# Row statistics dealt out piece by piece, token loads moved to the head of each product, weighting one step later, and output splits placed behind P1's copies

## The chip, the core and the metric

The kernel runs on one core of a Trainium2 chip. The metric is the device time of one execution in microseconds (us). Before the change three runs took 2683.50, 2684.97 and 2689.05 us, with a median of 2684.97.

## The reference

Input x has 2 sequences of 2048 tokens with 2048 features, all in fp32. The output is the residual of x with an attention layer and a routed feed-forward layer on the normalised tokens:

```python
xn = _layernorm(x, axis=-1)
# attention, one head of width 512
qkv = jnp.einsum('bsc,cf->bsf', xn, Wqkv) + bqkv          # 2048 -> 3 x 512
attn = softmax(jnp.einsum('bqd,bkd->bqk', q, k) * scale)
att = jnp.einsum('bqd,dc->bqc', jnp.einsum('bqk,bkd->bqd', attn, v), Wo) + bo
# feed-forward, 64 experts of rank 8
scores = (xn @ Wq_w.T) @ keys.T                           # 2048 -> 16 -> 64
top_vals, top_idx = jax.lax.top_k(scores, 16)             # softmax over the 16, scattered to a gate of 64
z = (xn @ A_w.T) * gate                                   # 2048 -> 512, 8 features to an expert
ffn = z @ B_w.T * SCALING                                 # 512 -> 2048
return x + att + ffn
```

## The kernel before, in words

**Tiling.** Tokens are taken in 8 blocks of 512 (four blocks to a sequence), each block as four tiles of 128 rows. Each fp32 product is made from three passes: an operand is cast to fp32r (`hi`, `split_hi`, L122, on ScalarE, ACT), what the cast dropped is kept as a second operand (`lo`, `split_lo`, L125, on VectorE, DVE), and three of the four combinations are accumulated in PSUM (`product`, L130). So each weight piece and each activation goes through a DMA, a cast on ACT and a subtraction on DVE before TensorE (PE) can use it. Seven PSUM banks serve the products (`acc`), one the small transposes (`misc`).

**Stages.** (1) `first_block` and the features of block 0: 12 feature tiles of 48 matmuls, 128x512 each (to 204 us). (2) Block 1: `values(1)` (L285) makes the values and the router's input in two halves h, each over eight weight pieces c2 with 24 matmuls of 128x264, in four banks; then 12 feature tiles (to 399 us). (3) Blocks 2 to 7 in pairs, `PAIRS` j = 1 to 3, by a seven-product scheme over the pair: phases P1, P2, P6, P5, P3, P7, P4 in this order (`phase`, L740). A phase has seven items: six feature tiles of 24 matmuls (5.44 us at the steady pitch of 227 ns) and one item "V" for the values. (4) Attention in 128 steps of 12 + 12 matmuls: `score(s)`, and after a lag `soft` (exponential and split) and `weigh`. (5) The output projection, 8 groups q of seven `STEPS`, again P1 to P4 by name, in `multiply` and `combine`, with `moving` bringing the output weights.

**Normalising.** Layernorm needs each row's mean and reciprocal deviation. `stats_steps` (L201) makes the steps for one block: for each of four row tiles it loads the rows (`xs`, L214) and takes `bn_stats` (L195) and an aggregate (L198) on DVE; then `finish_` copies the means into `mr` (L220), prepares the variance (L188) on DVE, raises it to -0.5 on GpSimd (POOL, L189), transposes `mr` on PE (L223), copies it out of PSUM on ACT (L225), writes it to DRAM (L227) and reads it back spread over all partitions (`mb`, L229). `norm` (L243 on, blocks 0 and 1) and `x_steps` (L608 loads of `xq`, L615 and L616 the arithmetic, later blocks) apply it to the transposed tokens.

**What sets the order of work.** Each engine works through its instructions in the order in which the scheduler puts them. `last` holds the latest instruction recorded on a queue under a key, and `behind(...)` issues what is in its body after that one. SyncE (SP) issues all the DMAs, so its queue is the one DMA queue. Weights of the phases are fetched two pieces ahead (`fetch`, L579; its DMA is L592), and a `fetch` sets `last["sp"]` and `last["dve"]`. The side work of a phase is a list of steps that `beside` (L647) returns; `phase` deals it out evenly over the seven items, each step behind SP, PE and DVE. There the token loads of the next product are steps like the others. In P2 and P3 item V comes first; its results feed `router` and `choose` (top 16 of 64 by repeated maxima on DVE, L447) behind items 0 and 1. In `values(1)` a statistics step comes with every third piece; `values_out` copies a half's banks out on DVE (`vs`, L125). Feature tiles of blocks 0 and 1 take side steps from the table `todo`. Steps are merged evenly by `mixed`.

**Attention's lag.** `LAG` = 20: step s scores tile s, softens tile s-18 and weighs tile s-20. A block is 16 steps. `maxes(blk)` takes a block's row maxima on DVE (to `mq`, L947), `spread` transports them with one matmul (L957). `combos` (L1076 on DVE, inputs `xz`) makes sums for the output stage in the same loop.

**Output stage.** P1's result `ps` is copied to `u` by ACT (L1139), and P2 then accumulates onto the same bank. In the last group of the first column half (q = NG-1), `moving(1, ...)` loads the second half's output weights, and the list `more` holds their splits (`wb`, from `wo<-tw_d`, L122 and L125), made a step after their loads.

Of the kernel before, what the change touches and what calls it, by code (L numbers as in the profile page):

```python
# [8 lines left out]
F32 = mybir.dt.float32  # L9
# [7 lines left out]
P = 128  # L17
C = 2048
# [13 lines left out]
LAG = 20  # L32
# [31 lines left out]
def attn_ffn_kernel(ctx: ExitStack, tc, x, xT, wq, wv, wob, bqk, bv, bo, keysT, out):  # L64
# [136 lines left out]
    def stats_steps(i, r, cols, out):  # L201

        part = {}

        def rows(t):
            if t == 0:
                part["mv"] = const.tile([P, NT, 2], F32, name="mv", bufs=2)
            mv = part["mv"]
            st = const.tile([P, 4, 6], F32, name="st6", bufs=2)
            parts = 0  # L210
            for c in range(C // cols):
                xs = r([P, cols], F32, "xs")
                r0 = i * T + t * P
                nc.sync.dma_start(xs, x[r0 : r0 + P, c * cols : (c + 1) * cols])  # L214
                parts = row_stats(mv[:, t, :], [xs], parts, st)

        def finish_():
            mv = part["mv"]
            mr = const.tile([P, 2, NT], F32, name="mr", bufs=2)
            nc.vector.tensor_copy(mr[:, 0, :], mv[:, :, 0])  # L220
            rstd(mr[:, 1, :], mv[:, :, 1], NT)
            pt = misc([2 * NT, P])
            nc.tensor.transpose(pt, mr.rearrange("p a t -> p (a t)"), ident)  # L223
            ts = const.tile([2 * NT, P], F32, name="ts", bufs=1)
            nc.scalar.copy(ts, pt)  # L225
            sd = dram.tile([2 * NT, P], F32, name=f"sd{i}")
            nc.sync.dma_start(sd, ts)  # L227
            mb = r_mb([P, 2, T], F32, "mb")
            nc.sync.dma_start(  # L229
                mb.rearrange("p a t -> p (a t)"),  # L230
                sd.rearrange("a b -> (a b)").unsqueeze(0).to_broadcast([P, 2 * T]),
            )
            out[i] = mb

        return [lambda t=t: rows(t) for t in range(NT)] + [finish_]
# [49 lines left out]
    def values(i, xn, steps):  # L285
        qr = router_in()
        for h in range(2):
            ps = [acc() for t in range(NT)]
            for c2 in range(NCH // 2):
                wh = wv_piece(h, c2)  # L290
                for cc in range(2):
                    c = 2 * c2 + cc
                    for t in range(NT):
                        sl = slice(t * P, (t + 1) * P)
                        product(
                            ps[t][:, :VH], lambda a: xn[c][:, a, sl], lambda b: wh[:, b, cc, :],
                            c == 0, c == NCH - 1,
                        )
                if steps and c2 % 3 == 1:
                    with behind("sp", "pe"):  # L300
                        steps.pop(0)()
            flush()
            for t in range(NT):
                values_out(i, t, h, r_ev, qr, ps[t])
        return qr
# [341 lines left out]
    def beside(j, ph):  # L647
# [4 lines left out]
        if ph == "P1":  # L652
            t3 = sum_steps(j, nc.vector, b01, b11, b01, ALU.subtract)
            if j > PAIRS[0]:
                return mixed(
                    split_steps(j, "P2", *b10), x_steps(j, *b01)[1], x_steps(j, *b11)[1], t3
                )
            q = [x_steps(j, *b) for b in (b10, b01, b11)]
            loads = [st for k in range(3) for st in q[k][0]]
            return loads + mixed(q[0][1], split_steps(j, "P2", *b10)) + mixed(q[1][1], q[2][1])  # L660
        if ph == "P2":
            t3 = sum_steps(j, nc.vector, b01, b11, b01, ALU.subtract) if j == PAIRS[0] else []
            return mixed(
                t3, sum_steps(j, nc.vector, b00, b01, b00, ALU.add), split_steps(j, "P6", *b00)
            )
        if ph == "P6":
            return mixed(
                sum_steps(j, nc.vector, b10, b10, b00, ALU.subtract),
                sum_steps(j, nc.vector, b00, b11, b00, ALU.subtract), split_steps(j, "P5", *b00),
                s0[:NT] if more else [],  # L670
            )
        if ph == "P5":
            steps = mixed(split_steps(j, "P3", *b11), s1[:NT] if more else [])
            return steps[:2] + s0[NT:] + steps[2:] if more else steps
        if ph == "P3":
            n = x_steps(j + 1, *b00) if more else ([], [])
            steps = mixed(split_steps(j, "P7", *b01), n[1][:2])
            return n[0] + (s1[NT:] if more else []) + steps
        if ph == "P7":
            n = x_steps(j + 1, *b10) if more else ([], [])  # L680
            return n[0] + mixed(split_steps(j, "P4", *b10), n[1][:2])
        if more:
            return (
                x_steps(j + 1, *b01)[0] + x_steps(j + 1, *b11)[0] + x_steps(j + 1, *b00)[1][2:]
                + mixed(split_steps(j + 1, "P1", *b00), x_steps(j + 1, *b10)[1][2:])
            )
        return []
# [52 lines left out]
    def phase(j, ph, n):  # L740

        steps = beside(j, ph)
# [64 lines left out]
    for i in range(2):  # L807
        if i:
            s2 = stats_steps(2, r_xs, 1024, mbs)
            qr = values(i, xn, s2[:NT])  # L810
# [6 lines left out]
        if i == 0:  # L817
            s1 = stats_steps(1, r_xs, 1024, mbs)
            todo = {3: s1[:2], 4: s1[2:4], 7: s1[4:]}
        else:  # L820
            s3, q = stats_steps(3, r_xs, 1024, mbs), x_steps(1, 0, 0)
            todo = {1: s3[:2] + s2[4:], 2: s3[2:4], 4: q[0], 5: s3[4:], 6: q[1][:2], 7: q[1][2:]}
# [311 lines left out]
    def combine(q, step, t, ps):  # L1134
        if step == "P1":
# [3 lines left out]
            nc.scalar.copy(u, ps)  # L1139
# [39 lines left out]
    for s in range(NSTEP + LAG):  # L1179
# [10 lines left out]
        if LAG <= s < LAG + 8 * 2 * ND and s % 8 == 4:  # L1190
            n = (s - LAG) // 8
# [8 lines left out]
        if 0 <= s - LAG + 2 < NSTEP:  # L1200
            soft(s - LAG + 2)
# [32 lines left out]
    for q in range(2 * NG):  # L1234
# [4 lines left out]
        for n, step in enumerate(STEPS):  # L1239
# [16 lines left out]
            m = n + 7 * q - 7 * (NG - 1)  # L1256
            if 0 <= m <= 7:
                for _, split in more:
                    split()
# [45 lines left out]
```

## Time and profile before

| | us |
|---|---|
| runs, median of three | 2684.97 |
| the profiled execution | 2687.31 |
| its span | 2685.5 |
| PE busy | 2637.3 |
| DVE busy | 1804.4 |
| ACT busy | 859.8 |
| POOL busy | 571.7 |

The mean granted TensorE clock was 0.992 of full speed. The chain of work that ended last was 75% PE by its own instructions, 1% DVE, 1% issue. Of PE's instructions the three-pass products at L130 hold 52% of that chain, the output products at L1127 22%. DMA moved 530 MB, 198 GB/s on the mean; a 512-KB load of tokens (`xq`) landed 6.2 us after its issue by the median, and a 512-KB weight piece of the phases after 3.6 to 3.9 us.

How to read it: a row of the waits says which PE instruction waited for whose result, for how long in total, how often, and the longest. In a timeline a row is a run of like instructions on one engine, with its start, its length, and in brackets how long the engine was idle before it and what ended the idling. A row can hold several instructions (x3), and its times then include the gaps between them.

### The profile page before, as it was taken

What the parts mean: (1) busy time and instruction counts of PE and PEld (TensorE: products, weight loads), DVE (VectorE), ACT (ScalarE), POOL (GpSimd) and SP (SyncE); (2) the same over time, 40 slices, a digit from 0 to 9 for tenths busy, and PEclk for the clock granted to TensorE, in tenths of its full rate; (3) what the DMA queues carried; (4) which work ended last, traced back from release to release, by engine and by line L of the source; (5) the groups of instructions that cost most, each with busy time, mean ns of one, the idle gap of its engine ahead of it and who ended that gap; (6) DMA issues with size and microseconds to landing.
All of it is one profiled execution on the core that took longest, in us unless ns stands there. A gap on an engine that the chain in (4) does not pass through costs nothing.

```text
span 2685.5 us, 33806 instructions
## 1 busy us (share of the span) xinstructions
PE 2637.3 (98%) x12875; PEld 2230.5 (83%) x12875; DVE 1804.4 (67%) x2481; ACT 859.8 (32%) x1271; POOL 571.7 (21%) x355
## 2 busy tenths in 40 slices
PE   8997999999999999999999999999999999989999
PEld 8887888888888888888888888888878888878887
DVE  7567647967878678756544775456657776786675
ACT  4332323323333333323233433334434222232221
POOL 2321420001000000000100101000000655565554
PEclk9998999999999999999999999999999999999999
DMA  7676874667646684536835476534457544664543
GB/s 261 233 271 229 280 261 168 228 211 266 216 143 211 220 291 158 167 118 212 289 114 179 156 259 243 197 116 142 145 180 247 163 163 160 200 202 163 181 155 105
DMA packets 243363, 530.42 MB, mean 198 GB/s; under 512 B 21576, under 2 KB 87168, under 8 KB 243200
## 3 DMA queue, kind: packets, MB, share of 16 engines
q1 hardware_dynamic: 243200, 528.26, 58.5%
q8 instruction: 101, 1.65, 0.2%
q14 instruction: 62, 0.51, 0.1%
HBM read 393.80 MB, written 134.38 MB: 197 GB/s over the span
## 4 chain that ended last, share of the span: by engine, by line
PE 75%; DVE 1%; issue 1%; DMA 0%; POOL 0%; ACT 0%; SPq 0%; DVEq 0%; POOLq 0%; ACTq 0%
PE acc L130 52%; PE acc L1127 22%; DVE wb L125 0%; DMA xz<-oz_d 0%; DMA wo<-tw_d 0%; DVE s L125 0%; PE misc L957 0%; DVE xz L1078 0%; DVE xo L1116 0%; POOL mr L189 0%; PE misc L997 0%; PE misc L998 0%; PE misc L435 0%; DVE xz L1076 0%; DVE xz L1079 0%
## 5 line engine op out<-in xcount | busy, mean ns | idle before, releaser
L130 PE MATMUL acc<-t,pw 128*128 128x512 f32 x3024 | 697.0, 391 | 1.1 <-DVE pw L125 1.1
L130 PEld LDWEIGHTS acc<-t,pw 128*128 128x128 f32 x3024 | 567.6, 188 | 119.4 <-DVE pw L125 1.3
L1127 PE MATMUL acc<-wb,s 128*128 128x512 f32 x2688 | 612.3, 390 | 8.6 <-ACT u L1139 8.6
L1127 PEld LDWEIGHTS acc<-wb,s 128*128 128x128 f32 x2688 | 506.0, 188 | 114.3 <-ACT u L1139 9.0
L130 PE MATMUL acc<-ph,vt 128*128 128x512 f32 x1536 | 369.9, 391 | 0.6 <-DVE ph L125 0.6
L130 PE MATMUL acc<-qt,kt 128*128 128x512 f32 x1536 | 366.1, 389 | 0.0
L130 PEld LDWEIGHTS acc<-ph,vt 128*128 128x128 f32 x1536 | 289.2, 189 | 63.2 <-DVE ph L125 1.4
L130 PEld LDWEIGHTS acc<-qt,kt 128*128 128x128 f32 x1536 | 288.1, 188 | 60.2 <-issue 0.2
L1111 POOL TENSOR_TENSOR xo<-xo,bo_bc 128x512 f32<-128x512 f32 x128 | 205.9, 1615 | 590.5 <-DMA xo<-in_x 555.0
L122 ACT CAST pw<-pw 128x1024 fp32r<-128x1024 f32 (+1 forms) x168 | 177.8, 1058 | 414.5 <-PE acc L130 295.3
L125 DVE TENSOR_TENSOR pw<-pw 128x1024 fp32r<-128x1024 f32 (+1 forms) x168 | 210.8, 1255 | 84.9 <-ACT pw L122 79.7
L130 PE MATMUL acc<-xh,wh 128*128 128x512 f32 x1152 | 263.7, 390 | 0.0
L130 PEld LDWEIGHTS acc<-xh,wh 128*128 128x128 f32 x1152 | 215.6, 188 | 45.0
L130 PEld LDWEIGHTS acc<-pw,t 128*128 128x128 f32 x2016 | 245.7, 188 | 4.4 <-DVE pw L125 3.2
L130 PE MATMUL acc<-pw,t 128*128 128x264 f32 x2016 | 246.4, 283 | 3.0 <-DVE pw L125 3.0
L122 ACT CAST s<-xz 128x1024 fp32r<-128x1024 f32 x112 | 118.0, 1054 | 378.2 <-PE acc L1127 311.6
L125 DVE TENSOR_TENSOR s<-xz,s 128x1024 fp32r<-128x1024 f32 x112 | 165.7, 1479 | 49.2 <-ACT s L122 49.1
L125 DVE TENSOR_TENSOR ph<-sp,ph 128x512 fp32r<-128x512 f32 x128 | 94.2, 745 | 102.4 <-ACT ph L122 101.9
L929 DVE TENSOR_TENSOR M<-M,sp 128x512 f32<-128x512 f32 x112 | 80.1, 715 | 121.3 <-ACT sp L923 121.2
L505 POOL TENSOR_TENSOR zt<-zt,g 128x512 f32<-128x512 f32 x24 | 38.1, 1595 | 477.1 <-DMA g<-gd 242.7
L923 ACT COPY sp<-acc 128x512 f32<-128x512 f32 x128 | 74.7, 585 | 201.1 <-PE acc L130 201.0
L125 DVE TENSOR_TENSOR wh<-wu,wh 128x512 fp32r<-128x512 f32 x96 | 89.1, 941 | 71.7 <-ACT wh L122 71.5
(147 smaller groups left out, 2382.0 us busy)
## 6 DMA issues: line engine op xcount, KB each, us to landing
vt<-v_d SPq DMA_DIRECT2D x128, 512.0 KB, 3.5
pw<-sq_d SPq DMA_DIRECT2D x72, 512.0 KB, 3.9
xz<-oz_d SPq DMA_DIRECT2D x64, 512.0 KB, 4.5
xo<-in_x SPq DMA_DIRECT2D x128, 256.0 KB, 3.6
out_y<-xo SPq DMA_DIRECT2D x128, 256.0 KB, 2.7
pw<-in_wq SPq DMA_DIRECT2D x54, 512.0 KB, 3.6
wu<-in_wq SPq DMA_DIRECT2D x48, 512.0 KB, 6.3
xq<-in_xT SPq DMA_DIRECT2D x48, 512.0 KB, 6.2
```

Source lines behind the costliest of these rows:

```text
L122: nc.scalar.copy(hi, src)
L125: return (eng or nc.vector).tensor_tensor(lo, src, raw(hi), ALU.subtract)
L130: last["pe"] = nc.tensor.matmul(ps, st(a_), mv(b_), start=first and n == 0, stop=end and n == 2)
L505: nc.gpsimd.tensor_tensor(zt, zt, gx[n], ALU.mult)
L923: nc.scalar.copy(st, ps)
L929: nc.vector.tensor_tensor(M[blk], M[blk], st, ALU.max)
L1111: nc.gpsimd.tensor_tensor(xs, xs, bo_bc[q // (NB // 2 * NH), c], ALU.add)
L1127: nc.tensor.matmul(ps, st[a_][:, kk, sl], mv[b_], start=not more and kk == 0 and n == 0, stop=kk == ND - 1 and n == 2, skip_group_check=more,)
```

## The change

- `stats_steps` gives two steps per row tile (with 1024 columns to a load) rather than one, with the loads running ahead by the number of buffers less one, and then two last steps: `chain` (the DVE and POOL part of `finish_`) and `spread_out` (from the PE transpose on).
- `values(1)` takes its statistics in the second half only, one step to each weight piece, and behind DVE as well.
- The `todo` tables of the feature tiles deal the smaller steps over more tiles, and move `chain` and `spread_out` of block 1 to tiles 7 and 8, those of block 2 to tiles 0 and 1, those of block 3 to tiles 5 and 6.
- `beside` returns loads and steps apart, and `phase` issues all the loads at its start, behind the last weight DMA. In P5 and P3 `chain` is the first step, and `spread_out` comes after six and three more steps. P1 of the first pair merges its steps in another order without the loads.
- `LAG` is 21 with the softmax at s-18 as before, so only `weigh` moves, by one step; `combos` keeps its place.
- In the output stage ACT's copy of `u` is recorded as `last["act"]`; the splits in `more` are made one step later and behind it.

```diff
@@ -29,7 +29,7 @@
 EPS = 1e-5
 SCALE = 1.0 / (512.0 ** 0.5)
 LOW = -3.0e38
-LAG = 20
+LAG = 21
 
 
 def raw(ap):
@@ -200,27 +200,37 @@
 
     def stats_steps(i, r, cols, out):
 
-        part = {}
-
-        def rows(t):
-            if t == 0:
-                part["mv"] = const.tile([P, NT, 2], F32, name="mv", bufs=2)
-            mv = part["mv"]
-            st = const.tile([P, 4, 6], F32, name="st6", bufs=2)
-            parts = 0
-            for c in range(C // cols):
-                xs = r([P, cols], F32, "xs")
+
+        v, tiles = {}, {}
+        per = C // cols
+
+        def load(k):
+            if k < NT * per:
+                t, c = divmod(k, per)
+                tiles[k] = r([P, cols], F32, "xs")
                 r0 = i * T + t * P
-                nc.sync.dma_start(xs, x[r0 : r0 + P, c * cols : (c + 1) * cols])
-                parts = row_stats(mv[:, t, :], [xs], parts, st)
-
-        def finish_():
-            mv = part["mv"]
-            mr = const.tile([P, 2, NT], F32, name="mr", bufs=2)
-            nc.vector.tensor_copy(mr[:, 0, :], mv[:, :, 0])
-            rstd(mr[:, 1, :], mv[:, :, 1], NT)
+                nc.sync.dma_start(tiles[k], x[r0 : r0 + P, c * cols : (c + 1) * cols])
+
+        def rows(k):
+            t, c = divmod(k, per)
+            if k == 0:
+                v["mv"] = const.tile([P, NT, 2], F32, name="mv", bufs=2)
+                for n in range(len(r.tags) - 1):
+                    load(n)
+            if c == 0:
+                v["st"] = const.tile([P, 4, 6], F32, name="st6", bufs=2)
+                v["parts"] = 0
+            load(k + len(r.tags) - 1)
+            v["parts"] = row_stats(v["mv"][:, t, :], [tiles[k]], v["parts"], v["st"])
+
+        def chain():
+            mr = v["mr"] = const.tile([P, 2, NT], F32, name="mr", bufs=2)
+            nc.vector.tensor_copy(mr[:, 0, :], v["mv"][:, :, 0])
+            rstd(mr[:, 1, :], v["mv"][:, :, 1], NT)
+
+        def spread_out():
             pt = misc([2 * NT, P])
-            nc.tensor.transpose(pt, mr.rearrange("p a t -> p (a t)"), ident)
+            nc.tensor.transpose(pt, v["mr"].rearrange("p a t -> p (a t)"), ident)
             ts = const.tile([2 * NT, P], F32, name="ts", bufs=1)
             nc.scalar.copy(ts, pt)
             sd = dram.tile([2 * NT, P], F32, name=f"sd{i}")
@@ -232,7 +242,7 @@
             )
             out[i] = mb
 
-        return [lambda t=t: rows(t) for t in range(NT)] + [finish_]
+        return [lambda k=k: rows(k) for k in range(NT * per)] + [chain, spread_out]
 
     mbs = {}
 
@@ -296,9 +306,9 @@
                             ps[t][:, :VH], lambda a: xn[c][:, a, sl], lambda b: wh[:, b, cc, :],
                             c == 0, c == NCH - 1,
                         )
-                if steps and c2 % 3 == 1:
-                    with behind("sp", "pe"):
-                        steps.pop(0)()
+                if h == 1:
+                    with behind("sp", "pe", "dve"):
+                        steps[c2]()
             flush()
             for t in range(NT):
                 values_out(i, t, h, r_ev, qr, ps[t])
@@ -651,40 +661,39 @@
         s0, s1 = stat_steps.get(2 * j + 2), stat_steps.get(2 * j + 3)
         if ph == "P1":
             t3 = sum_steps(j, nc.vector, b01, b11, b01, ALU.subtract)
+            n10, n01, n11 = x_steps(j, *b10), x_steps(j, *b01), x_steps(j, *b11)
             if j > PAIRS[0]:
-                return mixed(
-                    split_steps(j, "P2", *b10), x_steps(j, *b01)[1], x_steps(j, *b11)[1], t3
-                )
-            q = [x_steps(j, *b) for b in (b10, b01, b11)]
-            loads = [st for k in range(3) for st in q[k][0]]
-            return loads + mixed(q[0][1], split_steps(j, "P2", *b10)) + mixed(q[1][1], q[2][1])
+                return [], mixed(split_steps(j, "P2", *b10), n01[1], n11[1], t3)
+            return (
+                n10[0] + n01[0] + n11[0],
+                mixed(n10[1], split_steps(j, "P2", *b10)) + mixed(n01[1], n11[1]),
+            )
         if ph == "P2":
             t3 = sum_steps(j, nc.vector, b01, b11, b01, ALU.subtract) if j == PAIRS[0] else []
-            return mixed(
+            return [], mixed(
                 t3, sum_steps(j, nc.vector, b00, b01, b00, ALU.add), split_steps(j, "P6", *b00)
             )
         if ph == "P6":
-            return mixed(
+            return [], mixed(
                 sum_steps(j, nc.vector, b10, b10, b00, ALU.subtract),
                 sum_steps(j, nc.vector, b00, b11, b00, ALU.subtract), split_steps(j, "P5", *b00),
-                s0[:NT] if more else [],
+                s0[:-2] if more else [],
             )
         if ph == "P5":
-            steps = mixed(split_steps(j, "P3", *b11), s1[:NT] if more else [])
-            return steps[:2] + s0[NT:] + steps[2:] if more else steps
+            steps = mixed(split_steps(j, "P3", *b11), s1[:-2] if more else [])
+            return [], s0[-2:-1] + steps[:6] + s0[-1:] + steps[6:] if more else steps
         if ph == "P3":
             n = x_steps(j + 1, *b00) if more else ([], [])
             steps = mixed(split_steps(j, "P7", *b01), n[1][:2])
-            return n[0] + (s1[NT:] if more else []) + steps
+            return n[0], s1[-2:-1] + steps[:3] + s1[-1:] + steps[3:] if more else steps
         if ph == "P7":
             n = x_steps(j + 1, *b10) if more else ([], [])
-            return n[0] + mixed(split_steps(j, "P4", *b10), n[1][:2])
+            return n[0], mixed(split_steps(j, "P4", *b10), n[1][:2])
         if more:
-            return (
-                x_steps(j + 1, *b01)[0] + x_steps(j + 1, *b11)[0] + x_steps(j + 1, *b00)[1][2:]
-                + mixed(split_steps(j + 1, "P1", *b00), x_steps(j + 1, *b10)[1][2:])
-            )
-        return []
+            return x_steps(j + 1, *b01)[0] + x_steps(j + 1, *b11)[0], mixed(
+                x_steps(j + 1, *b00)[1][2:], split_steps(j + 1, "P1", *b00)[:2],
+            ) + mixed(split_steps(j + 1, "P1", *b00)[2:], x_steps(j + 1, *b10)[1][2:])
+        return [], []
 
     XU, YU, XV, YV = {}, {}, {}, {}
 
@@ -739,7 +748,10 @@
 
     def phase(j, ph, n):
 
-        steps = beside(j, ph)
+        loads, steps = beside(j, ph)
+        with behind("sp"):
+            for st in loads:
+                st()
         ops = [tsp[j, ph, cp] for cp in range(NCP)]
         qr, gx = None, {}
         i = 2 * j + (ph in ("P3", "P7"))
@@ -807,7 +819,7 @@
     for i in range(2):
         if i:
             s2 = stats_steps(2, r_xs, 1024, mbs)
-            qr = values(i, xn, s2[:NT])
+            qr = values(i, xn, s2)
         nxt, gx, held, vsum = None, {}, {}, None
         pairs = [(0, True), (1, False), (2, True), (3, False), (4, True), (5, False)]
         if i:
@@ -816,10 +828,14 @@
         todo = {}
         if i == 0:
             s1 = stats_steps(1, r_xs, 1024, mbs)
-            todo = {3: s1[:2], 4: s1[2:4], 7: s1[4:]}
+            todo = {3 + k: s1[2 * k : 2 * k + 2] for k in range(4)}
+            todo |= {7: s1[8:9], 8: s1[9:]}
         else:
             s3, q = stats_steps(3, r_xs, 1024, mbs), x_steps(1, 0, 0)
-            todo = {1: s3[:2] + s2[4:], 2: s3[2:4], 4: q[0], 5: s3[4:], 6: q[1][:2], 7: q[1][2:]}
+            todo = {1 + k: s3[2 * k : 2 * k + 2] for k in range(4)}
+            todo |= {0: s2[8:9], 5: s3[8:9] + q[1][:1], 6: s3[9:] + q[1][1:2], 7: q[1][2:]}
+            todo[1] = s2[9:] + todo[1]
+            todo[3] = q[0] + todo[3]
         for k, (fp, fh, summed) in enumerate(order):
             f = tile_of(fp, fh)
             with behind("pe"):
@@ -1136,7 +1152,7 @@
             if t == 0:
                 unit[0] = r_u([P, NA, T], F32, "u")
             u = U[q, t] = unit[0][:, t, :]
-            nc.scalar.copy(u, ps)
+            last["act"] = nc.scalar.copy(u, ps)
             return
         u = U[q, t]
         if step == "P2":
@@ -1187,8 +1203,8 @@
         if s % 8 == 3 and pending:
             with behind("sp"):
                 flush()
-        if LAG <= s < LAG + 8 * 2 * ND and s % 8 == 4:
-            n = (s - LAG) // 8
+        if 20 <= s < 20 + 8 * 2 * ND and s % 8 == 4:
+            n = (s - 20) // 8
             with behind("sp"):
                 combos(n // ND, n % ND)
         if 1 <= blk <= NB:
@@ -1197,8 +1213,8 @@
             if k == (1 if blk < NB else 2):
                 with behind("pe"):
                     spread(blk - 1)
-        if 0 <= s - LAG + 2 < NSTEP:
-            soft(s - LAG + 2)
+        if 0 <= s - LAG + 3 < NSTEP:
+            soft(s - LAG + 3)
         if 0 <= s - LAG < NSTEP:
             weigh(s - LAG)
         e = s - NSTEP
@@ -1253,10 +1269,11 @@
                 ahead(7 * q + n + 3)
             if q == NG - 1 and n == 0:
                 load_bo(1)
-            m = n + 7 * q - 7 * (NG - 1)
+            m = n + 7 * q - 7 * (NG - 1) - 1
             if 0 <= m <= 7:
-                for _, split in more:
-                    split()
+                with behind("act"):
+                    for _, split in more:
+                        split()
                 more = [moving(1, STEPS[m], kk) for kk in range(0, ND, 2)] if m < 7 else []
                 for load, _ in more:
                     load()
```

## The prediction

> **What bounds the kernel now.** I read the page's busy shares first, then the list of TensorE's waits, and then, at each wait, the order of work on the engine that released it.
>
> ```profile
> PE 2637.3 (98%) x12875; PEld 2230.5 (83%) x12875; DVE 1804.4 (67%) x2481; ACT 859.8 (32%) x1271; POOL 571.7 (21%) x355
> ```
>
> TensorE (PE) works for 98% of the span, and the change touches no matmul. So only PE's holes can be won, with the half-clock stretches behind them. The list of PE's waits names nearly all:
>
> ```profile
> PE acc L130 <- DVE vs L125: 10.9, 1, 10.9
> PE acc L1127 <- ACT u L1139: 8.6, 1, 8.6
> PE misc L223 <- POOL mr L189: 5.0, 2, 2.5
> ...
> PE acc L130 <- DVE pw L125: 4.1, 2, 3.0
> PE misc L957 <- DVE mq L947: 3.9, 1, 3.9
> PE acc L130 <- DVE wh L125: 3.5, 1, 3.5
> ```
>
> (Columns: total us, times, longest.) On PE's timeline they start running again at 243.05 (after 10.92), 2379.72 (8.57), 613.20 and 929.19 (2.50 each), 447.15 and 459.67 (2.97, 1.12), 2009.58 (3.95) and 222.22 (3.47). The remaining holes lie in the start-up and stay. A hole costs more than its length where the clock drops. To price a place I therefore take its real length less matmuls times the steady pitch (227 ns for 512 columns, 121 ns for 264):
>
> - second block's values, 203.96 to 267.38: 63.4 us for 384 matmuls of 264 columns, which need 46.7. Lost: 16.7.
> - 613 and 929: the 48 matmuls behind each hole took 12.28 and 12.50 us (chain of waits), against 10.9. Lost: 2.5+1.4 and 2.5+1.6, together 8.0.
> - 2379: the hole 8.57 and some 2.4 behind it at half clock. Lost: 11.0.
> - 447 and 459: 4.1, no drop of the clock. 2009: 8.2 with its half clock.
>
> **Second block's values (243).** DVE's timeline of before:
>
> ```profile
> 234.17 1.29 DVE L195 BATCH_NORM_STATS2 st<-xs 128x6 f32<-128x512 f32 x2 [0.38 <-DMA xs<-in_x]
> 235.37 0.69 DVE L125 TENSOR_TENSOR wh<-ws,wh 128x528 fp32r<-128x528 f32 x1
> 240.18 0.69 DVE L195 BATCH_NORM_STATS2 st<-xs 128x6 f32<-128x512 f32 x1 [4.11 <-DMA xs<-in_x]
> 240.79 0.69 DVE L125 TENSOR_TENSOR wh<-ws,wh 128x528 fp32r<-128x528 f32 x1
> 241.40 1.28 DVE L195 BATCH_NORM_STATS2 st<-xs 128x6 f32<-128x512 f32 x2
> 242.59 1.04 DVE L125 TENSOR_TENSOR vs<-acc,vs 128x248 fp32r<-128x248 f32 x3
> ```
>
> The reader is to see that the evictions of the first half (vs) stand behind statistics that wait 4.11 us for their rows. The second half needs a bank of the first, so PE stops. The change removes the statistics from the first half and puts one 1024-column step behind each weight piece of the second, its loads two ahead. The count of loads and bn_stats is the same. In the built order of the changed kernel the first vs has ahead of it, counted from the last normalised operand (xh): seven splits of weights (0.61 us each in a run: 4.3), 13 bn_stats (7.8) and three aggregates (0.5), together 12.6 us of DVE work. Statistics are thus still ahead of the evictions, and this edit doesn't clear them. In before the last xh was at 222.6. Two things pull it: the first half loses six bn_stats (3.6 us) and the 4.71-us wait for xs at 202.44, but normalising starts about 10 us later, because the transpose of the block's means moves from 149.4 to about 160.4 (48 matmuls on). DVE had other waits in that stretch (3.07 at 192, 1.01 at 170) which can take up a part. I put the last xh at 219 to 221, the first vs at 234 to 236. PE used up its banks at 243.05-10.92=232.1, and would at 228.7 without the 3.47-us hole at 222, which is of the same backlog. A hole of about 5.7 us then ends near 234.4, and with 2.3 at half clock 8.0 are lost instead of 16.7: gain 8.6. Bounds: 3 (normalising is not made up, vs at 239) to 16 (no hole).
>
> **First pair's P1 (447, 459).** Of 12 loads of tokens (xq) 11 now issue together, ahead of the weight piece that went out at 399.48; in before they were spread over three pieces, DVE idled 4 to 5 us at a time before 420, and the normalising then stood back to back ahead of weight splits until 458. It will start near 405, so the 4.1 goes. The price lies on SP, the only DMA queue: ten 512-KB transfers of before landed between 406.65 and 418.58, or 1.33 us each. The first of the burst issues at 392.0 and lands near 398; eleven more put the weight piece at 412.6 to 414. PE needs it at 415.6, less 1.05 (cast) and 1.2 (split): 413.3. Stall 0 to 1.5, so gain 4.1-1.0=3.1 (bounds -1 and 4.1). In the P4s seven or eight loads go ahead of a piece that lands near 681 and is needed at 684.2; in P3 and P7 four or two. These cost nothing as long as a transfer takes 1.33; at 2.0 they would run about 2 us late each.
>
> **The transposes (613, 929).** The 2.25-us POOL power stands just ahead of PE's transpose, and waits on DVE copies held up behind the top-16 steps. The change puts DVE's and POOL's part at the head of phase P3, the transpose after three more steps: 48 matmuls (10.9 us) behind the top-16's instead of 24. What could be late next is P3's first split, behind two copies of 0.17: nothing. POOL's queue holds only the memset of qr before it, and POOL was idle for 11.28 us ahead of the power in before. Here the Trainium skill speaks against the gain ("TensorE: Matmul & The Clock Gate", section "🎯 Why this matters for your kernels"): the clock falls back to half only after a whole window of about 3 us idle. By the rule these two holes are worth 2x2.50=5.0. The rows say otherwise: the clock was granted at half for 3.41 us from 613.0 and from 930.4, and 48 matmuls took 1.4 and 1.6 too long, while after 3.47 (at 222) and 2.97 (at 447) it did not drop. So length alone doesn't decide. I take the rows' 8.0 (bounds 5.0, and 8.0 as there is no more to win).
>
> **Output splits (2379).** ACT's timeline:
>
> ```profile
> 2375.96 1.04 ACT L122 CAST s<-xz 128x1024 fp32r<-128x1024 f32 x1 [4.29 <-DVE xz L1079]
> 2378.13 1.04 ACT L122 CAST wb<-wo 128x1024 fp32r<-128x1024 f32 x1 [1.12 <-DMA wo<-tw_d]
> 2379.09 1.07 ACT L1139 COPY u<-acc 128x512 f32<-128x512 f32 x2
> 2380.04 1.05 ACT L122 CAST s<-xz 128x1024 fp32r<-128x1024 f32 x1
> ```
>
> P2 accumulates onto P1's bank and so needs u, and u stood behind two casts that waited for DVE and for a DMA. The changed order has the u copies ahead of both. The splits come one step (5.4 us) later and are first used five steps on, so that is covered. Gain 11.0; if the casts' own lateness then reaches PE, 8.5.
>
> **LAG.** Softmax stays at its step and the weighting runs one step later. In the steady blocks mq is ready 5.3 us ahead of its transpose, and stays so; probabilities are held one step longer, which the buffers cover in the built order. At the tail the transpose (L957) stands after 53 matmuls (of 227 ns) instead of 50, and its chain of maxes is the same length: gain 0.8 (bounds -1 and 1.5), and the 3.95 stays.
>
> **The sum.** 8.6+3.1+8.0+11.0+0.8=31.5. New small stalls that I can't place (weights behind the first block's later loads, where two pieces near 195 have under 3 us to spare): -1.5. Gain 30.0. The profiled execution took 2687.31 (span 2685.5 and 1.8 around it), giving 2657.3; it lies 2.3 above the runs' median of 2684.97, so against that 2655.0.
>
> **The rivals.**
> - A, every named hole goes, the values' too: that adds up to 8 in values, 1 in P1 and 1.5 of small stalls: 2644.5. For it: the half-clock loss goes with the hole. Against: 12.6 us of DVE work ahead of vs. Chance 0.14.
> - B, the values' hole stays nearly, as normalising starts 10 us late and statistics still stand ahead: gain 1 in place of 8.6, so 2662.6. For it: DVE's order. Chance 0.16.
> - C, bursts of tokens delay weights: at 2.0 us a transfer P1's piece is 8 late and costs 3 at half clock, both P4s 2 to 4: 8.6 less, and P1's gain of 3.1 gone too, 14 or so: 2669. Against: 1.33 measured. Chance 0.11.
> - D, slower: in the values' second half each of eight weight splits stands behind a statistics step on DVE, and the last loads stand behind rows' loads on SP that wait for a buffer. If rows were fetched one after another instead of three in flight, a piece would take 6.2 (the median landing) plus 1.2, 7.4 instead of 2.9, with half the clock after every hole: 8x4.5=36 and up to 23 for 192 matmuls at twice 121 ns. The other gains are 22.9-1.5 and the old loss 16.7, so it turns the sign when the half loses more than 38; at 59 the time is 2706 (2685-21+59-17). Against: three buffers, so about 2.5 a step. Chance 0.04.
> - E, the edits move nothing that PE waits for, the holes only wander: 2685. Against: the u copies visibly change places. Chance 0.03.
>
> **How the numbers follow.** The likeliest case, 0.52, is 2655, its own range 2648 to 2662. I leave out the faster part of A (below 2641) and C beyond 2669, D and E: range 2641 to 2669. This kernel's measurement can tell about 0.2% (5.4 us) from no change. Faster 0.93, same 0.03, slower 0.04.
>
> **What would show it.** Waits on POOL mr and on ACT u gone; no half clock near 613, 930 and 2374; the hole at 2009 still about 4; the values' hole at 4 to 8, ended by vs; no wait on pw near 447, but perhaps one of at most 1.5 near 415. I am wrong if a wait on wh or pw of over 5 us appears at a burst, or if PE's holes shrink and its busy time grows.

## The result, and the profile after

Ten runs of the changed kernel took 2674.65 to 2680.78 us, median 2676.26; ten of the kernel before had a median of 2684.56. The ratio is 0.997, with a 95% interval of 0.996 to 0.998: faster, by 8.3 us instead of the 30.0 forecast. The profiled execution took 2676.42 (span 2674.6), 10.9 less than that of before. The forecast time was 21 us too low, and below even the fastest run.

The waits of TensorE (PE) in the changed kernel, columns as before: total us, times, longest.

```profile
PE acc L130 <- DVE vs L125: 8.5, 1, 8.5
PE acc L130 <- DVE pw L125: 6.6, 1, 6.6
...
PE acc L1143 <- ACT u L1155: 5.7, 1, 5.7
PE misc L973 <- DVE mq L963: 3.8, 1, 3.8
```

The transposes' waits for GpSimd (POOL) and that for VectorE's (DVE) wh are gone. The waits for vs and for u are shorter, not gone. That for pw is longer than the two of before together, and it lies elsewhere, at 412.57: a wait of over 5 us on pw at a burst was the prediction's own sign of being wrong. A wait of 0.9 on t, at 543.40, is new.

The span cut into stages at PE's marks: first matmul of block 1's values, of its features, of the pairs' phases, of the first P2, of the attention, start of the output. Each number is a difference of starts in the trace. (With LAG 20 six of the output's matmuls run among the last of the attention; there the start of the output is put six matmuls, 1.36 us, ahead of the seventh.)

| stage, us | before | after | gain | forecast |
|---|---|---|---|---|
| up to the values | 203.96 | 205.90 | -1.94 | 0 |
| values of block 1 | 63.41 | 57.18 | 6.2 | 8.6 |
| features of block 1 | 131.92 | 131.88 | 0.0 | 0 |
| first pair's P1, with the wait at the head of P2 | 60.38 | 64.95 | -4.6 | 3.1 |
| the other phases | 887.90 | 880.92 | 7.0 | 8.0 |
| attention | 713.33 | 712.26 | 1.1 | 0.8 |
| output (to PE's end) | 620.53 | 617.41 | 3.1 | 11.0 |

The gains sum to 10.9, the difference of the two profiled executions. In the first stage the change only deals block 1's statistics out otherwise. Its -1.94 is within the scatter: in the fifteen profiled executions told of here that have this stage as in the changed kernel, it took 203.0 to 206.3. So two stages carry most of the shortfall: P1 (7.7) and the output (7.9).

**P1.** SyncE's (SP) timeline, and the chain of waits in the changed kernel, from 391 on (start, length, what):

```profile
389.08 9.54 SPq L618 DMA_DIRECT2D xq<-in_xT  x11
399.56 0.43 SPq L602 DMA_DIRECT2D pw<-in_wq  x1
```

```profile
391.15 8.34 DMA xq<-in_xT
...
399.56 10.63 DMA pw<-in_wq
...
410.21 1.05 ACT pw L122
...
411.29 1.24 DVE pw L125
...
412.57 1.65 PE acc L130 x3
```

The weight piece behind the eleven token loads landed at 410.19, cast and split follow at once, and PE starts with them. It had begun the phase at 394.96 and stopped at 406.0, after two items. The pieces were forecast to be used in the order in which they are issued. The built order of both kernels shows otherwise: the fourth piece's load stands ahead of the third's on SP, because the third's waits for PE to free its buffer (in before PE released it at 399.47, and it went out at 399.48). The piece behind the burst is the third, needed 5.4 us sooner than the forecast had it. The landing itself was nearly as forecast: 15.2 us after the start of the phase, where 412.6 to 414 were 13.3 to 14.7 after it. With the need at 413.3-5.4=407.9, the same working would have given a stall of 5 to 6 us; it was 6.57. The clock was granted at half for 6.83 us from 410.58, 4.8 of them behind the stall, so some 2.4 more were lost.

The trace also shows why a load at the end of a full queue takes 10.6 us. No DMA of this queue goes out before the one eight places ahead of it has landed: the token load of 391.15 landed at 399.50, and the weight piece, eight places behind it, was issued at 399.56. Some eight transfers of 1.35 us then lie between its issue and its landing.

**The output.** ScalarE's (ACT) timeline in the changed kernel:

```profile
2358.97 1.06 ACT L122 CAST wb<-wo 128x1024 fp32r<-128x1024 f32 x1 [2.39 <-DMA wo<-in_wob]
2359.94 1.04 ACT L122 CAST s<-xz 128x1024 fp32r<-128x1024 f32 x1
2366.54 1.05 ACT L122 CAST wb<-wo 128x1024 fp32r<-128x1024 f32 x1 [5.56 <-DMA wo<-in_wob]
2367.49 1.04 ACT L122 CAST s<-xz 128x1024 fp32r<-128x1024 f32 x1
2368.44 1.06 ACT L1155 COPY u<-acc 128x512 f32<-128x512 f32 x2
```

Of the two casts that the forecast saw ahead of u, only the one of weights (wb) is behind it now, with the other one of its step. The cast of s is still ahead of u: 59 casts of s and 26 of wb come before this u in before, 59 and 24 in the changed kernel. And a step later is a step later for all: the weight casts of the step before, until now done in time, have become the last ones ahead of u, and the second of them waited 5.56 us for its load. PE had been out of work since 2363.3. The stall of 5.73 and some 2.1 at half clock behind it make 7.8, where before lost 11.0.

**The values.** DVE's timeline in the changed kernel, and SP's:

```profile
229.55 1.27 DVE L195 BATCH_NORM_STATS2 st<-xs 128x6 f32<-128x512 f32 x2
232.82 0.71 DVE L125 TENSOR_TENSOR wh<-ws,wh 128x528 fp32r<-128x528 f32 x1 [2.00 <-ACT wh L122]
233.45 1.28 DVE L195 BATCH_NORM_STATS2 st<-xs 128x6 f32<-128x512 f32 x2
...
237.16 0.71 DVE L125 TENSOR_TENSOR wh<-ws,wh 128x528 fp32r<-128x528 f32 x1 [2.14 <-ACT wh L122]
...
238.39 1.04 DVE L125 TENSOR_TENSOR vs<-acc,vs 128x248 fp32r<-128x248 f32 x3
```

```profile
228.80 2.38 SPq L212 DMA_DIRECT2D xs<-in_x  x2
231.27 0.86 SPq L264 DMA_DIRECT2D ws<-in_wv  x2
```

The last xh came at 220.3, within the forecast 219 to 221 (218.4 with the 1.9 of the start taken off). From its end to the first vs it was 17.4 us where 12.6 of work were counted. The rest is idling, 2.00 and 2.14 of it for casts of weight pieces whose loads stand on SP behind loads of rows that wait for a buffer. So the hole was 8.5 instead of 5.7.

### The profile page after: what moved, and what is told of

The parts are those of the page before. It is cut to its first block, busy times and chain, and to the rows that moved or that the text cites. A ratio compares the mean times of both kernels' runs of the same rounds, so it can differ in the third digit from the quotient of the medians.

```text
span 2674.6 us, 33809 instructions
## 1 busy us (share of the span) xinstructions
PE 2636.0 (99%) x12875; PEld 2229.5 (83%) x12875; DVE 1815.5 (68%) x2481; ACT 859.6 (32%) x1271; POOL 567.3 (21%) x355
## 4 chain that ended last, share of the span: by engine, by line
PE 91%; DVE 4%; DMA 3%; issue 1%; ACT 0%; POOL 0%; SPq 0%; DVEq 0%; ACTq 0%; POOLq 0%
PE acc L130 69%; PE acc L1143 21%; DMA xs<-in_x 1%; DMA wo<-in_wob 0%; DVE xc L254 0%; DMA pw<-in_wq 0%; DVE st L195 0%; DMA xc<-in_xT 0%; DMA xz<-oz_d 0%; DVE wb L125 0%; DMA xq<-in_xT 0%; DVE xq L645 0%; DVE wh L125 0%; DMA ws<-in_wv 0%; DVE pw L125 0%
## 5 line engine op out<-in xcount | busy, mean ns | idle before, releaser
L125 DVE TENSOR_TENSOR pw<-pw 128x1024 fp32r<-128x1024 f32 (+1 forms) x168 | 216.2, 1287 | 75.1 <-ACT pw L122 72.9
L125 DVE TENSOR_TENSOR s<-xz,s 128x1024 fp32r<-128x1024 f32 x112 | 172.4, 1540 | 46.4 <-ACT s L122 46.3
```

Source lines behind the costliest of these rows:

```text
L125: return (eng or nc.vector).tensor_tensor(lo, src, raw(hi), ALU.subtract)
```

## The experiments

All are made from the changed kernel and compared with the kernel before on the same chip. The time is the median; "saves" and "costs" are against the changed kernel's 2676.3. The kernel before had medians of 2684.56 to 2686.11 beside the different groups of runs, so a saving or cost of 1 to 2 us says nothing; there the stage's time in the trace is the better reading.

**P1's token loads in three groups.**

```diff
+        if ph == "P1" and j == PAIRS[0]:
+            later = {0: loads[4:8], 1: loads[8:]}
+            loads = loads[:4]
...
                 fetch(n + 1)
+            with behind("sp"):
+                for st in later.get(m, []):
+                    st()
```

> The changed kernel, but the twelve token loads of the first pair's P1 in three groups of four: the first at the start of the phase as now, the second behind the fetch of item 0, the third behind that of item 1. Against the changed kernel (2676.3). Theory, the third weight piece stands behind eleven token loads on the one DMA queue: it is then issued some 10 us earlier relative to TensorE, the 6.6-us wait for pw and the 6.8 us at half clock behind it go, 9 us less, about 2667. Rival, the burst is innocent and VectorE's normalising ahead of the split is late: the wait on pw stays at 5 to 7 us, 2675 to 2677. In between: the wait goes but the waits near 447 of the kernel before (4.1 us together) come back, about 2671.

2664.32, ratio 0.9922 (0.9908 to 0.9936): saves 12.0. SP's timeline of this kernel shows the third piece ahead of the second group, 0.2 us after the start of the phase (393.7) instead of 4.6:

```profile
387.74 2.28 SPq L618 DMA_DIRECT2D xq<-in_xT  x3
393.91 0.34 SPq L602 DMA_DIRECT2D pw<-in_wq  x1
394.30 2.25 SPq L618 DMA_DIRECT2D xq<-in_xT  x4
```

PE's waits for pw are gone altogether, those of before at 447 and 459 too, and P1 takes 55.84: 4.5 less than before, where the forecast had 3.1 after taking 1.0 off for the burst. So the gain in P1 was real, and the burst cost 9.1 in that stage (the rest of the 12.0 lies in stages that this edit doesn't touch, 1.7 of it in the first). It is the loads, not DVE.

**Output splits two steps later.**

```diff
-            m = n + 7 * q - 7 * (NG - 1) - 1
+            m = n + 7 * q - 7 * (NG - 1) - 2
```

> The changed kernel, but the loads and splits of the second column half's output weights one more step later (two steps behind the kernel before). Theory, the copies of u stand on ScalarE behind the last cast of the step before, which waits for its DMA (landed 2366.5, TensorE out of work at 2363.3): the cast ahead of u then belongs to a load issued a step earlier in that chain, so the 5.7-us wait and about 1.7 us behind it at half clock go, about 2669. Rival, this chain of load, cast, split and freed buffer simply runs slower than TensorE, so whatever stands ahead of u comes late: the wait stays at 4 to 6 us, 2674 to 2677.

2669.86 (0.9927 to 0.9952): saves 6.4. ACT's timeline has u as soon as P1 gives it:

```profile
2359.29 0.58 ACT L1155 COPY u<-acc 128x512 f32<-128x512 f32 x1
2361.90 0.59 ACT L1155 COPY u<-acc 128x512 f32<-128x512 f32 x1 [2.03 <-PE acc L1143]
```

PE doesn't wait for u any more, and the output takes 612.96, 7.6 less than before and 4.5 less than in the changed kernel. It isn't the whole 11: two waits on DVE's s (2.9 us together) come up instead.

**Output part taken back** (splits one step earlier, not behind u).

> The changed kernel with the second half's output splits where they were (one step earlier and not held behind the copies of u). The two traces give the part 8.6+2.4 less 5.7+1.7, some 3.5: 2680, with the wait on u at 8 to 9 us. Rival, the place of the output hole depends on what arrives there and the part is worth the forecast 11: 2687; or nothing: 2676.

2677.55 (0.9954 to 0.9979). The wait for u was 8.95 and the output took 620.92, 3.5 more than in the changed kernel, as the two traces had it. The runs' medians differ by only 1.3, which alone would show nothing. The stage's time does: in ten profiled executions with the output as changed it was 616.1 to 618.5.

**Chain and transpose of the means put back in P5 and P3.**

```diff
-            return [], s0[-2:-1] + steps[:6] + s0[-1:] + steps[6:] if more else steps
+            return [], steps[:2] + s0[-2:] + steps[2:] if more else steps
...
-            return n[0], s1[-2:-1] + steps[:3] + s1[-1:] + steps[3:] if more else steps
+            return n[0], s1[-2:] + steps if more else steps
```

> The changed kernel, but in P5 and P3 the means' chain and its transpose are together again at the places of the kernel before. Theory, that part won 8.0: the two 2.5-us waits of the transpose for GpSimd come back near 609 and 925 with their 3.4 us of half clock each, 2684. Rival by length of the holes alone: 5.0, 2681. Rival, the part won nothing because the time was given back later in the phases: 2676.

2676.95 (0.9957 to 0.998): nothing lost, against the theory. POOL's timeline shows why: the power ran at 591.43, ahead of the memset of qr and of the top-16's steps.

```profile
591.43 1.01 POOL L189 TENSOR_TENSOR mr<-ve,nhalf 128x4 f32<-128x4 f32 x1 [45.13 <-DVE ve L188]
600.35 0.21 POOL L292 MEMSET qr<- 128x128 f32 x1 [7.91 <-PE misc L438]
```

**P3's token loads back in the list as well**, P5 as in the last.

```diff
-            return n[0], s1[-2:-1] + steps[:3] + s1[-1:] + steps[3:] if more else steps
+            return [], n[0] + ([lambda: [st() for st in s1[-2:]]] if more else []) + steps
```

> The changed kernel, but in P3 the four token loads are again steps of the list, the means' chain and transpose one step behind them, and in P5 chain and transpose together at the place of before: P3's order on TensorE is that of the kernel before. The run with chain and transpose alone put back had lost nothing. Theory now, what won the 8 us is that the four loads no longer take places in the list ahead of the chain, so that it comes ahead of the top-16 steps: the two 2.5-us waits for GpSimd come back, 8 us more than the changed kernel, 2684. Rival, they went because the statistics are dealt out in smaller steps with loads ahead, and stay away: 2676 to 2677. By the length of the holes alone 2681.

2683.68 (0.9984 to 0.9997): costs 7.4. Both waits of 2.49 us are back, and the power is behind the memset:

```profile
602.00 0.21 POOL L292 MEMSET qr<- 128x128 f32 x1 [54.07 <-PE misc L438]
613.45 2.25 POOL L189 TENSOR_TENSOR mr<-ve,nhalf 128x4 f32<-128x4 f32 x1 [11.24 <-DVE ve L188]
```

Only one of the two holes brought the half clock back, and the phases behind P1 took 7.1 more than in the changed kernel. `phase` deals the list out evenly over seven items. Four loads ahead of the means' step put it into the fourth item of the phase, behind `choose`; without them it falls into the first two. So taking the loads out of the list is enough for this gain, whatever became of chain and transpose. That the new places of chain and transpose would have done it with the loads still in the list wasn't tried.

**LAG 20 again.**

> The changed kernel with the weighting two steps behind softmax again (LAG 20). The forecast gave this part 0.8: 2677. A rival: the probabilities' splits then have one step less to be ready and waits on ph appear through the attention, 2680 or more. Or it is nothing that can be measured: 2676.

2675.67 (0.9948 to 0.9975): nothing that can be measured. The attention took 711.91 against 712.26; over the fourteen profiled executions with LAG 21 it took 711.2 to 714.1, and the 713.33 of before lies among them.

**Block 2's statistics as before in the values product** (three steps of two loads in the first half, one in the second, behind SP and PE only).

> The changed kernel, with the statistics of block 2 again at three of the first half's pieces and one of the second's, not tied to VectorE (the loads still ahead by two). The values product of the two traces differs by 6.2 us. Theory, the dealing of this part won them: 63 us instead of 57.2, 2682. Rival, they came from the loads running ahead, or from the later means of block 1: 57 to 59, 2676 to 2678.

2676.39 (0.9956 to 0.9981), the values 55.28. So dealing the steps over the second half won nothing. The 6.2 came with what this run keeps, above all the loads two ahead and the later means of block 1. Which of them is open. The traces point to the loads: from 199 us to the first vs, DVE waited for rows (xs) 10.8 us in before, 3.1 in this run and 0.3 in the changed kernel. No run has the one without the other.

**Statistics of blocks 2 and 3 beside the features of block 1**, in two forms: left to the scheduler, and held behind the weight splits on DVE.

> The changed kernel, but no row statistics of block 2 in the values product of block 1: they are taken beside the feature tiles behind it (tiles 0 to 4), those of block 3 in tiles 3 to 8. Theory, the evictions of the first half stand behind statistics, whose rows and whose place on the DMA queue delay the last weight pieces: with none there the 8.5-us wait for vs goes or falls under 1 us, with its 10.2 us of half clock; 9 to 10 us less, about 2667. Rival, normalising of block 1, which starts later than before, sets the time of the evictions: the wait stays at 5 us or more, 2671 or above. A cost that could appear: waits for weights in the feature tiles behind, where seven more statistics steps now lie.

2674.92 (0.9941 to 0.9966), with a wait for vs of 7.8: inconclusive, since the scheduler had put three of the steps ahead of vs again.

> The changed kernel, but the row statistics of blocks 2 and 3 all beside the feature tiles 1 to 9 of block 1, and behind the latest weight split on VectorE too, so that in the built order only weight splits stand ahead of the first half's evictions (in the run with the statistics in the features, three of their steps had still been scheduled ahead of the evictions, and VectorE idled 5.1 us for rows there while the casts of vs were ready). Theory, statistics and their rows ahead of the evictions make the wait: it goes or falls under 1 us and the values product takes 47 to 48 us instead of 57.2; about 9 us less than the changed kernel (2676.3), 2667. Rival, normalising of block 1 is late itself: a wait of 3 us or more on wh or vs stays, 2671 or above.

2680.52 (0.9972 to 0.9986): costs 4.2. PE's waits:

```profile
PE acc L130 <- DVE wh L125: 14.0, 3, 9.0
...
PE acc L130 <- DVE vs L125: 1.1, 1, 1.1
```

The values took 47.75 us, the 46.7 that its matmuls need and the 1.1. So the statistics ahead of the evictions, with their rows, are the cause of that wait. But the features took 150.92 instead of 131.9, with 14.0 us of waits for weights (wh). Ahead of the split that ended the longest of them, DVE was idle for 6.01 us: ACT's cast waited for a weight load issued at 325.79, which landed at 332.50. There it is the queue of loads that is late, not DVE's time.

**Block 2's statistics behind the third eviction**, the rest as changed.

```diff
-                    with behind("sp", "pe", "dve"):
+                    with behind("sp", "pe", "dve", "vs"):
...
-        split_lo(vs[:, 1, n0:], v[:, n0:VH], vs[:, 0, n0:])
+        lo = split_lo(vs[:, 1, n0:], v[:, n0:VH], vs[:, 0, n0:])
+        if t == 2:
+            last["vs"] = lo
```

> The changed kernel, with the statistics of block 2 in the second half of the values product as now, but each also behind the third eviction of the first half on VectorE; the rest, block 3's and the feature tiles' steps too, as in the changed kernel. The run with all statistics behind the evictions and beside the features lost no time in the values product (47.9 us) but 19 in the features. Theory: the wait for vs goes (8.5 plus about 2 at half clock) and the features stay at 132 us, as their own steps are where they were: 2667. Rival, any placing behind the evictions pushes weight splits of the features behind rows on VectorE and on the DMA queue: the values product takes 48, the features 137 or more, 2671 to 2676.

2677.77 (0.996 to 0.9983). Values 46.94, features 140.88. ACT's timeline shows where it was given back:

```profile
267.52 0.38 ACT L122 CAST vs<-acc 128x264 fp32r<-128x264 f32 x1 [13.05 <-DMA v_d<-vs]
```

The second half's fourth eviction waits for the buffer of its first, which stands on DVE behind block 3's statistics; ACT stood 13 us with the router's copy queued behind it.

**Those behind the second half's evictions too**, and block 2's transpose two tiles later.

> The changed kernel with the statistics of block 2 behind the third eviction of the first half, the side steps of the feature tiles (block 3's statistics among them) behind the third eviction of the second half, and the transpose of block 2's means two tiles later (tile 3). In the run with only the first of these the values product took 47.1 us, but ScalarE then stood 13 us behind the second half's fourth eviction, as VectorE had block 3's statistics ahead of the second half's third, and TensorE waited 6.8 us at the transpose for a copy on ScalarE. Theory: with these behind as well the gain of 9 to 10 us stays, features 132 to 134 us, 2667. Rival, the steps' rows and DVE time don't fit anywhere near without a stall: features 137 or more, 2671 to 2677.

2677.47 (0.9959 to 0.998). Values 52.49 and features 133.76 make 186.3, 2.8 less than the changed kernel; but P1's wait for pw grew from 6.6 to 11.7. PE came to the phase earlier (391.2 instead of 395.0), and the piece behind the burst was no sooner (411.5, against 410.2).

**Repairs together.** P1 and output:

> The changed kernel with two of the repairs together: the first pair's P1 loads in three groups, the output weights' splits two steps later. They lie 1900 us apart, so the gains of 12.0 and 6.4 should add up: 2658. If they share something (a state of the DMA queue that is carried on), less: 2662.

2663.30 (0.9909 to 0.9933): more than either end expected, and only 1.0 below P1's repair alone. In its profiled execution the wait for vs was 11.8, which is scatter, and the output took 614.57, with four waits on s: the repair there saved 2.2 against P1's alone (616.81), not 4.5. Why it was worth less isn't known.

> The changed kernel with the repairs of P1 and the output and the statistics behind the third eviction. If the last is worth 9 alone, 2649; if it gives its gain back in the features, 2657 to 2660.

2663.54 (0.9906 to 0.9933), again above both ends expected. Values 52.72 and features 136.21, against 57.18 and 131.88 in the changed kernel: what the values won (4.5) came back in the features (4.3).

> The changed kernel with that, P1's loads in three groups and the output splits two steps later. P1 with output gave 2663.3; with another 9 to 10 it should take 2654. If the values' gain is given back, 2661 to 2664.

2667.03 (0.9916 to 0.9942). With P1's burst gone too, the features took 140.19: again most of what the values won (47.91) came back, and 2.4 us of waits for pw in P1 with it. So the best versions are P1's loads in groups, alone (2664.3) or with the later output splits (2663.3, and 2663.5 with the statistics behind the third eviction); their intervals don't tell them apart.

## Why the prediction was wrong

- **P1 (forecast 3.1, measured -4.6).** The failed step is "PE needs it at 415.6": the piece behind the burst was the third and not the fourth, was needed 5.4 us sooner, and PE stalled for 6.57 where 0 to 1.5 were forecast. The price of the transfer was right: between the landings of the third token load of the group (398.14) and the last (408.93) the trace has eight transfers, 1.35 us each. Rival C had the mechanism, but priced it at 2.0 us a transfer; it decides at 1.33 too, once the piece is the third. (C's sum is also off: 8.6 and 3.1 make 11.7, not 14.) Shown by the run with three groups.
- **Output (11.0, 3.1).** The failed step is "the changed order has the u copies ahead of both". The weight cast moved behind u, the cast of s did not, and the weight casts of the step before took the place ahead, as their loads had moved as well: u waited for a load, and PE 5.73 us for u. The fallback of 8.5 was not enough of a bound. Shown by the run with two steps, where the cast of s is still ahead of u and PE doesn't wait.
- **Values (8.6, 6.2).** The mechanism on which the size rested was right (the hole is ended by vs, with statistics ahead of it), but DVE's idling for weights between the counted steps, 4.1 us, was left out. What won the 6.2 was misjudged: not the dealing of the steps, as putting it back cost nothing. And the wait is of uneven length: in seven further profiled executions with this part as changed (all but those that move block 2's statistics) it was 7.4 to 11.8, with the stage at 56.5 to 60.7.
- **Transposes (8.0, 7.0).** Size about right (the new wait for t takes 0.9 of it in the same stage), credit wrong: the loads' leaving the list is enough for it, and the forecast priced that under the bursts alone. Put back, they cost 7.1 in the phases with holes of 5.0, so a hole did cost more than its length, as the rows had it.
- **LAG (0.8, 1.1 in the stage).** Nothing by the runs; the 1.1 is within the stage's scatter.
- **The base.** The profiled execution of before lay 2.75 above the ten runs' median, that of after 0.16: 2.6 of the 10.9 are only this.

The range failed because its lower half held every plan as working. A sum of five gains that each need their next wait to be absent should have kept a case in which two of them fail, and 2669 to 2677 was given to C alone at 0.11.

Open: what won the 6.2 in the values, and whether the work that the values' product sheds can be put anywhere before P1 at no cost. None of three placings kept the gain: it came back as time in the features, or as a longer wait in P1.

## What to carry to other kernels

Before a burst is put ahead of a load on a queue, read in the built order which consumer that load feeds and when; order of issue isn't order of use. When a step is moved, look at what then becomes last ahead of the waiter, with its landing time. And a list that is dealt out evenly moves all its members when some are taken out of it.

## What the runs showed of the hardware

A hole of 2.5 us on PE brought the half clock in both cases of before (613.0 and 930.4) but, in the run with P3's loads in the list, at one of two equal holes of 2.49 (616.2, not near 932). In the run with all statistics held behind the splits a hole of 2.83 brought it (299.7), while 2.97 and 3.47 in before had not. Length between 2.5 and 3.5 doesn't decide here.

The place of the hole does, and the sixteen traces show it. From 60 to 2655 us, every change of the granted clock in a trace lies on one grid of 3.413 us, to within 0.01 us. Cut each trace into the windows of its grid, and add up PE's idle time in each. After every window at full clock in which PE was idle for 1.83 us or less, the clock stayed (11,969 windows, 44 of them with more than 1 us idle). After every one with 1.96 or more it was at half in the next window (60 windows). What decides between the two figures no run shows. Here are a hole of 2.50 in before (613.2), which lies mostly within one window, and one of 2.49 in the run with P3's loads in the list (931.8), which a boundary cuts into 0.89 and 1.60. Each has its window and the next; the columns are the stretch, its length, PE's busy time with its instructions, then PE's weight loads, DVE, ACT and POOL, the granted clock, and the DMAs' share and rate:

```profile
609.55:612.97 3.42, 1.16 (x6) 0.61 (x4) 3.42 (x14) 1.35 (x2) 2.07 (x1) 1.00 0.65 255
612.97:616.38 3.41, 3.18 (x9) 2.50 (x10) 3.41 (x7) 0.77 (x2) 0.18 (x1) 0.50 0.31 58
...
930.25:933.66 3.41, 1.82 (x9) 1.52 (x10) 3.41 (x8) 1.23 (x3) 1.54 (x1) 1.00 0.47 163
933.66:937.07 3.41, 3.41 (x17) 2.83 (x16) 1.59 (x4) 0.00 (x0) 0.00 (x0) 1.00 0.79 221
```

The Trainium skill ("TensorE: Matmul & The Clock Gate", part "What's actually happening") has windows of 3413 ns that run freely, and the grid agrees with that. A whole idle window, which the prediction took from the same page as the condition, is not needed here: 1.96 us of 3.41 were enough.
